# A four-layer graph network: layer 0's denominators on all rows of a head, its outputs divided on the way out of PSUM

## The chip, the cores and the metric

The kernel runs on one core of a Trainium2 chip. The metric is the device time of one execution in microseconds. The median of three runs before the change is 3496.96 us (3496.95 to 3499.22).

## The reference

32 graphs of 512 nodes with 256 features, `x[32,512,256]`, and an adjacency `adj[32,512,512]` of zeros and ones, symmetric, with ones on the diagonal. Four layers follow each other, each as `x = layernorm(x + layer(x, adj))`. Layer 0 is what matters here (4 heads of 64 features; of its five edge types only type 1 occurs):

```python
h = einsum('bnd,hde->bhne', x, W)
weight = mask * (e_src[..., :, None] + e_dst[..., None, :])   # e_src, e_dst = h @ a_src, h @ a_dst
weight = where(adj == 0, NEG, leaky_relu(weight, 0.01))
attention = softmax(weight, axis=-1)
dst = einsum('bhij,bhje->bhie', attention, h) + bias
out = relu(dst) + h
out = per-head layernorm(out) * gamma + beta
```

Layer 1 is graph attention with ELU and one head, layer 2 a masked transformer block (8 heads of 32, feed forward 256 to 1024 to 256), layer 3 graph attention with one head and a leaky slope of 0.2. Everything is f32.

## The kernel before, in words

A graph's 512 nodes stand as R = 4 blocks of P = 128 rows; its features are D = 256 = K x 128 with K = 2. `graph(b)` is a Python generator that emits one graph's instructions, layer after layer, and yields between small units. Each unit has a place: `paced` (before each unit) yields `PERIOD * b + PLACES[stage][i]`, and `heapq.merge` over the 32 generators emits the units in the order of these places. PE's instructions stay in the order of emission (`manual_schedule` for PE). The other engines' orders are the tile framework's: its scheduler plans each engine's queue when the kernel is built, and the queues are then fixed. So a change of `PLACES` moves units of different graphs against each other on PE, and the other engines' queues follow. About seven graphs are in flight at a time. A unit whose place is lower than the current one is emitted at once: layer 0's first four (negative) places are that.

Buffers: PSUM has eight banks, one pool (`bank`). SBUF has a rotating pool for rows of 128x512 (`part`, nine buffers in stages of kind "a", to which layers 0 and 1 belong): gathered rows `gb`, masked weights `pt`, copies `back`, and layer 1's temporaries share it.

Layer 0 (`layer0`), for one graph:

- `h0p` (L104 in the profile, as every PE instruction goes through `product`): x times the weights, four row blocks. ACT takes three exponentials and a copy of each (L427 to L430). `hv[p, j, head, 0:64]` becomes (h + bias) times exp(0.01 e_dst), and column 64 of a head (`HC = 65`) that exponential itself (L431, L436 on DVE).
- `along` (`gp`): for each of four heads, PE transposes a broadcast column so that exp(-0.99 e_src) stands along the rows; ACT copies it out as `gb` (L349).
- Four steps over source blocks j: DVE makes the masked weights `pt` of the four heads, `max(gb, f) * at` (L407, `kept`), each 128x512. PE multiplies them: for each head two matmuls with 32 stationary columns (features 0 to 31 and 32 to 63) into `ops`, and then for each head one with 32 columns into `den`. A matmul of 32 columns writes 32 rows of a bank, and its place in the array (0, 32, 64 or 96) is where those rows begin. Before, a head's two matmuls go to rows 0 and 32, or 64 and 96, of one bank: heads 0 and 1 in the first bank, 2 and 3 in the second. The `den` matmul reads the last 32 columns of the head's 65, and only its last row is the denominator.
- ACT copies the three banks (`back`, L464). PE transposes them back in three units of four (`backp`): first `den`, of which DVE takes the reciprocals (L477), then the two output banks, which DVE divides while it takes the relu (L484).
- DVE adds h (L493), then the per-head layernorm (`head_layernorm`: L293 to L302 and ACT L299), gamma, x, and the layernorm over the row (`layernorm`, ACT L280).

`den` is also the name of attention's denominators in the profile (`den<-pr,ones`), `o` that of layers 1 and 3 (`o<-h,pt`). `s` and `cp` are attention's scores and products, `pr` its probabilities, L663 the adds of halves of `pr` for its denominators, `wop` the projection, `qkp` and `vp` q, k and v, `f1p` and `f2p` the feed forward. L680 adds `wop` to the residual, L273 and L274 are a layernorm's statistics (bn and their aggregation), L276 its shift, L560 the low part of q or k.

`rd` and `mvs` hold denominators' reciprocals and variances of a graph; four small DVE instructions at a graph's end (L825 to L829) check their bounds, on which a fallback path depends.

Of the kernel before, what the change touches and what calls it, by code (L numbers as in the profile page):

```python
# [9 lines left out]
F32 = mybir.dt.float32  # L10
# [4 lines left out]
ALU = mybir.AluOpType  # L15
# [11 lines left out]
PERIOD = 12054  # L27
PLACES = {
    "edges": [-3978, -1720, -957, -79],
    "x": [5375],  # L30
    "mask": [14366, 15324, 18155, 20933],
    "layer 0": [
        -33568, -33515, -33424, -32942, 5301, 7043, 7043, 7043, 8766, 10194, 11091, 11128,
        11993, 11993, 14391,
    ],
    "layer 1": [15460, 15460, 15555, 15555, 15555, 15555, 16382, 17321, 17344, 17344, 17355, 17355],
    "qkv": [18153, 18153, 22255, 22255, 23139, 24065, 25534, 25534, 25534, 25534, 25534],
    "attention": [
        -5960, -4506, -4506, -3927, 26460, 26497, 26497, 26593, 26886, 27435, 27446, 27462,
        28434, 28434, 28779, 29106, 29409, 30200, 31616, 32371, 34290, 34290,  # L40
    ],
    "projection": [34382, 34412, 34412, 34412, 34443],
    "feed forward": [
        36011, 36047, 37566, 38431, 38431, 38519, 38519, 38646, 38646, 38732, 38732, 39499,
        39499, 39646, 39646, 40873, 41200, 41449, 41464,
    ],
    "layer 3": [44919, 44919, 44969, 44969, 44969, 44969, 45682, 48065, 48065, 48065, 48422, 48422],
}
STAGES = {"edges": "a", "x": "a", "layer 0": "a", "layer 1": "a", "feed forward": "c", "layer 3": "c"}
ALL = mybir.DependencyInfo(mybir.DependencyClass.Sync, mybir.DependencyReason.DATA)  # L50
# [22 lines left out]
def fast_path(ctx: ExitStack, tc: tile.TileContext, a: dict, out: bass.AP, bad: bass.AP):  # L73
# [18 lines left out]
    NF = F // P  # L92
    QSCALE = DH**-0.5
    HC = HO + 1
    ND = R * (H + 2)
    NL = 6
    NV = R * (NL + H) + 2 * K

    nc.scalar.preload_act_table_set("natural_log_exp_and_others")
    const = ctx.enter_context(tc.tile_pool(name="const", bufs=1))  # L100
# [307 lines left out]
        return t  # L408


    def layer0(x, xt, at, rd, mv, var):
        h = buf([P, R, D], "h", "h0", 2)
        values = hv[:, :, :, :HO]
        ex = buf([P, 2, H, R], "ex", "ex0", 2)
        for r in range(R):
            yield
            p = bank("h0p")
            for k in range(K):
                product(nc.tensor.matmul,
                    p[:, : D + 2 * H],  # L420
                    xt[:, k, r * P : (r + 1) * P],
                    w0[:, k, :],
                    start=k == 0,
                    stop=k == K - 1,
                )
            s, d = p[:, D : D + H], p[:, D + H : D + 2 * H]
            nc.scalar.activation(ex[:, 0, :, r], s, AF.Exp, scale=-0.99)  # L427
            nc.scalar.activation(hv[:, r, :, HO], d, AF.Exp, scale=0.01)
            nc.scalar.activation(ex[:, 1, :, r], d, AF.Exp, scale=0.99)
            nc.scalar.copy(h[:, r, :], p[:, :D])  # L430
        nc.vector.tensor_add(  # L431
            values,
            h.rearrange("p r (h e) -> p r h e", h=H),
            bias0.rearrange("p (h e) -> p h e", h=H).unsqueeze(1).to_broadcast([P, R, H, HO]),
        )
        nc.vector.tensor_mul(values, values, hv[:, :, :, HO:].to_broadcast([P, R, H, HO]))  # L436
        gbs = []
        for hh in range(H):
            gbs.append((yield from along(ex[:, 0, hh, :].unsqueeze(2), "gb0")))
        den, *ops = (bank(name) for name in ("den0", "o0", "o0"))  # L440
        for j in range(R):
            pt = [kept("pt0", gbs[hh], at[:, j, :], ex[:, 1, hh, j : j + 1]) for hh in range(H)]
            yield
            for hh in range(H):
                for e in range(0, HO, DH):
                    product(nc.tensor.matmul,
                        ops[hh // 2][hh % 2 * HO + e : hh % 2 * HO + e + DH, :],
                        hv[:, j, hh, e : e + DH],
                        pt[hh],
                        start=j == 0,  # L450
                        stop=j == R - 1,
                    )
            for hh in range(H):
                product(nc.tensor.matmul,
                    den[hh * DH : (hh + 1) * DH, :],
                    hv[:, j, hh, HC - DH :],
                    pt[hh],
                    start=j == 0,
                    stop=j == R - 1,
                )  # L460
        back = []
        for i, o in enumerate((den, *ops)):
            t = part("back")
            nc.scalar.copy(t, o)  # L464
            back.append(t)
        y = sb.tile([P, R, D], F32, tag="y", name="y0", bufs=3)
        for i in range(1 + H // 2):
            yield
            p = bank("backp")
            for r in range(R):  # L470
                product(nc.tensor.transpose,
                    p[:, r * P : (r + 1) * P], back[i][:, r * P : (r + 1) * P], ident
                )
            if i == 0:
                rdh = rd.rearrange("p (i r h) -> p i r h", i=H // 2, r=R)
                for i in range(H // 2):
                    nc.vector.reciprocal(  # L477
                        rdh[:, i],
                        p.rearrange("p (r h e) -> p r h e", r=R, h=H)[
                            :, :, 2 * i : 2 * i + 2, DH - 1  # L480
                        ],
                    )
                continue
            nc.vector.scalar_tensor_tensor(  # L484
                y[:, :, (i - 1) * P : i * P].rearrange("p r (h e) -> p r h e", h=2),
                p.rearrange("p (r h e) -> p r h e", r=R, h=2),
                0.0,
                rdh[:, i - 1].unsqueeze(3).to_broadcast([P, R, 2, HO]),
                op0=ALU.max,
                op1=ALU.mult,  # L490
            )
        nc.vector.tensor_add(x, x, all_rows(bet0))
        nc.vector.tensor_add(y, y, h)  # L493
        head_layernorm(y, 1e-6, var)
        nc.vector.tensor_mul(y, y, all_rows(gam0))
        nc.vector.tensor_add(y, y, x)
        layernorm(y, 1e-5, mv[0])
        return y
# [257 lines left out]
        layernorm(x, 1e-5, mv[5])  # L756
        return x

    ends = [0, R * H, R * (H + 1), ND]
    def load_x(b):  # L760
        xt = sb.tile([P, K, N], F32, tag="xt0", name="xt0", bufs=1)
        nc.sync.dma_start(xt, a["xt"][b].rearrange("(k p) n -> p k n", p=P))
# [4 lines left out]
        nc.sync.dma_start(x, a["x"][b].rearrange("(r p) d -> p r d", p=P))  # L767
        return xt, x

    def layer0_all(b, x, xt, at, rd, mv, var):  # L770
        if b == 0:
            bcast(bet0, "bet0")
            bcast(gam0, "gam0")
        return (yield from layer0(x, xt, at, rd, mv, var))

    def layer1_all(b, x, at, rd, mv):
        if b == 0:
            weights13(w1g, "w1g", "a1")
        return (yield from layer1(x, at, rd, mv))
# [22 lines left out]
    def graph(b):  # L802
        yield PERIOD * b + PLACES["edges"][0]
        rd = sb.tile([P, ND], F32, tag="rd", name="rd", bufs=3)
        mvs = sb.tile([P, 2 * NL * R + H * R + 2 * K], F32, tag="mvs", name="mvs", bufs=3)
        mv = [mvs[:, 2 * i * R : 2 * (i + 1) * R].rearrange("p (r s) -> p r s", s=2) for i in range(NL)]
        tops = mvs[:, 2 * NL * R :]
        var, spread = tops[:, : H * R], tops[:, H * R :]
        rds = [rd[:, ends[i] : ends[i + 1]] for i in range(3)]
        if b == 0:  # L810
            xt, x = yield from paced(b, "x", load_x(b))
        at = yield from paced(b, "edges", mask(b))
        if b:
            xt, x = yield from paced(b, "x", load_x(b))
        x = yield from paced(b, "layer 0", layer0_all(b, x, xt, at, rds[0], mv, var))
        x = yield from paced(b, "layer 1", layer1_all(b, x, at, rds[1], mv))
        a2 = yield from paced(b, "mask", symmetric(b, at))
        qk = yield from paced(b, "qkv", qkv_all(b, x))
        ct = yield from paced(b, "attention", attention(qk, *a2, spread))
        y = yield from paced(b, "projection", attended_all(b, x, ct))  # L820
        x = yield from paced(b, "feed forward", feed_forward_all(b, x, y, mv))
        x = yield from paced(b, "layer 3", layer3_all(b, x, at, rds[2], mv))
        nc.sync.dma_start(out[b].rearrange("(r p) d -> p r d", p=P), x)
        okd, oks, okv = ok[:, :ND], ok[:, ND : ND + NL * R], ok[:, ND + NL * R :]
        nc.vector.scalar_tensor_tensor(okd, rd, RD_MIN, okd, op0=ALU.is_ge, op1=ALU.mult)  # L825
        nc.vector.scalar_tensor_tensor(okd, rd, RD_MAX, okd, op0=ALU.is_le, op1=ALU.mult)
        variances = mvs[:, 1 : 2 * NL * R : 2]
        nc.vector.scalar_tensor_tensor(oks, variances, VAR_MAX, oks, op0=ALU.is_le, op1=ALU.mult)
        nc.vector.scalar_tensor_tensor(okv, tops, VAR_MAX, okv, op0=ALU.is_le, op1=ALU.mult)  # L829
# [664 lines left out]
```

## Time and profile before

| What | Value |
|---|---|
| Median of three runs | 3496.96 us |
| The profiled execution, and its span | 3497.4 us, 3495.6 us |
| Granted TensorE clock, mean | 0.986 |
| DVE pt (L407), 128x512 | 768 of 742 ns |
| DVE add of halves (L663), 128x1024 | 384 of 1208 ns |
| DVE y + h (L493), 128x1024 | 32 of 1225 ns |
| DVE division with relu (L484), 128x512 from PSUM | 64 of 686 ns |
| DVE multiply (L611), 128x512 | 64 of 683 ns |
| DVE reciprocal of a bank's denominators (L477) | 64 of 175 ns |
| ACT copy of `den`, of `o` (L464), 128x512 | 32 of 585 ns, 64 of 595 ns |
| ACT Copy, Ln, Exp of attention's denominators (L606, L607, L608) | 64 each of 600, 637, 635 ns; reading the accumulator 196 and 199 ns more for L606 and L608 |
| DMA issue to landing: x, xt, adj, adjt | 5.1, 3.8, 5.0, 3.9 us |

A group in the profile is a line, an engine, an operation and tiles (out<-in), with the count, the busy time of all together and the mean duration of one; behind the bar stands how long its engine was idle before it and what ended that. Records on PE may overlap, so busy time is less than count times mean. In a timeline the columns are start, length, engine, line, operation, tiles, and how many instructions were merged. A matmul in f32 leaves two records, a transpose one.

### The profile page before, as it was taken

The page shows a single profiled execution, that of the slowest core. Times are in us where ns is not written, and L with a number is a line of the kernel's source. Part 1 is how long each engine was busy: PE and PEld are TensorE (multiplying, and loading weights), DVE is VectorE, ACT ScalarE, POOL GpSimd, SP SyncE. Part 2 cuts the span into 40 slices and gives each one's busy share as a digit, 9 for nine tenths or more (in the row PEclk, how much of TensorE's full clock was granted, in tenths as well). Part 3 has the DMA queues.
Part 4 walks back from the last instruction along what each step waited for, and adds up shares of the span by engine and source line. Part 5 has one row for each costly group of instructions (what it writes and reads, how often), then busy time and mean ns, then how long its engine had stood idle before and what let it go on. Part 6 is the DMA issues. An engine that isn't in the chain of part 4 may idle for free.

```text
span 3495.6 us, 51507 instructions
## 1 busy us (share of the span) xinstructions
PE 3397.5 (97%) x18342; PEld 2366.5 (68%) x18342; DVE 2888.4 (83%) x5178; ACT 2223.0 (64%) x5729; POOL 82.0 (2%) x171
## 2 busy tenths in 40 slices
PE   5799999999999999999999999999999999999986
PEld 3466667776667776667776667776666776666765
DVE  5778888888888888889888889888889888889863
ACT  3556667666667666667666667666667666666652
POOL 0000000000000000000000000000000000000000
PEclk8899999999999999999999999999999999999998
DMA  4334232333232333232333232334332333332220
GB/s 131 85 76 91 61 85 59 81 79 91 62 84 61 79 79 91 64 85 61 76 79 91 67 82 63 74 79 91 69 80 66 71 79 91 71 79 61 45 55 13
DMA packets 164038, 261.01 MB, mean 75 GB/s; under 512 B 20416, under 2 KB 56384, under 8 KB 163776
## 3 DMA queue, kind: packets, MB, share of 16 engines
q1 hardware_dynamic: 163776, 257.65, 32.0%
q8 instruction: 148, 2.42, 0.3%
q14 instruction: 114, 0.93, 0.1%
HBM read 106.57 MB, written 16.78 MB: 35 GB/s over the span
## 4 chain that ended last, share of the span: by engine, by line
PE 94%; DVE 3%; ACT 1%; issue 1%; DMA 1%; SPq 0%; POOL 0%; DVEq 0%; ACTq 0%; POOLq 0%
PE o L104 20%; PE f2p L104 13%; PE f1p L104 13%; PE s L104 8%; PE qkp L104 6%; PE cp L104 6%; PE den L104 5%; PE h3p L104 4%; PE wop L104 3%; PE h1p L104 3%; PE vp L104 3%; PE h0p L104 3%; PE gp L104 2%; PE backp L104 1%; PE xt3p L104 1%
## 5 line engine op out<-in xcount | busy, mean ns | idle before, releaser
L636 DVE TENSOR_TENSOR pr<-pr,a 128x1024 f32<-128x1024 f32 x384 | 454.7, 1217 | 185.4 <-ACT pr L633 185.4
L407 DVE SCALAR_TENSOR_TENSOR pt<-gb,ex,at 128x512 f32<-128x512 f32 x768 | 536.7, 742 | 42.0 <-ACT gb L349 31.6
L633 ACT ACTIVATE pr<-s 128x512 f32<-128x512 f32 x1024 | 545.3, 616 | 3.0 <-PE s L104 3.0
L104 PE MATMUL f2p<-wf,ft 128*128 128x256 f32 x2048 | 484.8, 379 | 5.4 <-ACT ft L706 5.2
L104 PE MATMUL f1p<-yt,wf 128*128 128x256 f32 x2048 | 483.8, 379 | 0.0
L104 PE MATMUL o<-h,pt 128*128 128x257 f32 x2048 | 476.5, 382 | 4.5 <-DVE pt L407 4.4
L104 PEld LDWEIGHTS o<-h,pt 128*128 128x128 f32 x2048 | 386.4, 190 | 99.1 <-issue 44.2
L663 DVE TENSOR_TENSOR pr<-pr 128x1024 f32<-128x1024 f32 x384 | 446.8, 1208 | 2.8 <-PE cp L104 2.8
L104 PEld LDWEIGHTS f2p<-wf,ft 128*128 128x128 f32 x2048 | 383.9, 190 | 63.4 <-ACT ft L706 9.8
L104 PEld LDWEIGHTS f1p<-yt,wf 128*128 128x128 f32 x2048 | 388.5, 190 | 55.0 <-DVE lo L560 0.5
L280 ACT ACTIVATE y<-y,rs 128x256 f32<-128x256 f32 x768 | 398.0, 593 | 17.1 <-DVE rs L276 17.1
L104 PE MATMUL s<-qk 128*128 128x512 f32 x1024 | 377.4, 470 | 4.6 <-DMA qk<-lo 3.8
L706 ACT ACTIVATE ft<-f1p,cols 128x256 f32<-128x256 f32 x512 | 217.0, 469 | 236.6 <-PE f1p L104 235.6
L273 DVE BATCH_NORM_STATS2 bn<-y 128x6 f32<-128x256 f32 x768 | 298.9, 410 | 5.6
L104 PE MATMUL o<-pt,hv 128*32 128x512 f32 x2048 | 286.5, 607 | 8.0 <-DVE pt L407 8.0
L265 ACT ACTIVATE rs<-mvs,eps1e-05_70 128x4 f32<-128x4 f32 x192 | 57.5, 300 | 326.7 <-DVE mvs L274 319.6
L104 PE MATMUL qkp<-xt,wqkv 128*128 128x512 f32 x512 | 240.5, 603 | 0.0
L104 PE MATMUL cp<-pr,v 128*32 128x512 f32 x2048 | 234.2, 595 | 1.4 <-DVE pr L636 1.4
L104 PEld LDWEIGHTS s<-qk 128*128 128x128 f32 x1024 | 189.3, 192 | 55.8 <-issue 27.7
L104 PEld LDWEIGHTS o<-pt,hv 128*32 128x32 f32 x2048 | 73.3, 110 | 179.6 <-issue 94.1
L559 ACT ACTIVATE hi<-qkp,cols 128x512 fp32r<-128x512 f32 x128 | 88.4, 691 | 164.1 <-PE qkp L104 162.1
L752 DVE RECIPROCAL rd<-o 128x1 f32<-128x1 f32 x128 | 21.5, 168 | 177.7 <-PE o L104 177.5
(139 smaller groups left out, 4881.9 us busy)
## 6 DMA issues: line engine op xcount, KB each, us to landing
qk<-hi SPq DMA_DIRECT2D x512, 128.0 KB, 3.4
qk<-lo SPq DMA_DIRECT2D x512, 128.0 KB, 3.5
adjt<-in_adjt SPq DMA_DIRECT2D x64, 512.0 KB, 3.9
adj<-in_adj SPq DMA_DIRECT2D x64, 512.0 KB, 5.0
xt<-in_xt SPq DMA_DIRECT2D x32, 512.0 KB, 3.8
x<-in_x SPq DMA_DIRECT2D x32, 512.0 KB, 5.1
out<-y SPq DMA_DIRECT2D x32, 512.0 KB, 4.5
wf<-in_w1t SPq DMA_DIRECT2D x1, 1024.0 KB, 9.8
```

The source lines that it names most:

```text
L104: latest[0] = what(*args, **kwargs).ins.name
L265: nc.scalar.activation(out, variance, AF.Ln, bias=eps[e])
L273: nc.vector.bn_stats(st[:, r, :], y[:, r, :])
L280: nc.scalar.activation(y[:, r, :], y[:, r, :], AF.Identity, bias=rs[:, 1, r : r + 1], scale=rs[:, 0, r : r + 1],)
L407: nc.vector.scalar_tensor_tensor(t, g, f, edges, op0=ALU.max, op1=ALU.mult)
L559: nc.scalar.activation(hi, p, AF.Identity, bias=bias)
L633: nc.scalar.activation(t[:, i, :], s, AF.Exp, scale=QSCALE)
L636: nc.vector.tensor_mul(t, t, edges)
L663: nc.vector.tensor_add(t, t, u)
L706: nc.scalar.activation(ft[:, f, :], p[:, f, :], AF.Relu, bias=bf1[:, ff + f : ff + f + 1])
L752: nc.vector.reciprocal(rd[:, r : r + 1], p[:, D : D + 1])
```

## The change

The two matmuls of a head now write the same 32 rows (those of the head) of the two output banks, so that features 0 to 31 of all heads stand in one bank and 32 to 63 in the other. The denominator's matmul has the column 64 of the head broadcast to 32 stationary columns: all 32 rows of a head in `den` are its denominator, and `den` lies like either output bank. ACT takes exp(-ln(den)) of the whole bank (`inv`), DVE multiplies both output banks by it as it moves them to SBUF, and PE transposes only these two. The relu and the addition of h are one DVE instruction, with strided views (`halves`). The bounds are checked on sums that ACT accumulates (`spread0`) instead of on 16 reciprocals. `mvs` has four buffers instead of three. Every list in `PLACES` is new, with one unit less in layer 0.

```diff
 PLACES = {
-    "x": [5375],
-    "mask": [14366, 15324, 18155, 20933],
+    "x": [6086],
+    "mask": [14366, 15398, 19563, 21001],
     "layer 0": [
-        -33568, -33515, -33424, -32942, 5301, 7043, 7043, 7043, 8766, 10194, 11091, 11128,
-        11993, 11993, 14391,
+        -36153, -36100, -36009, -36009, 2373, 3347, 3347, 3351, 8768, 10196, 11113, 11130,
+        13480, 14393,
     ],
...
-    "projection": [34382, 34412, 34412, 34412, 34443],
+    "projection": [34462, 34462, 35198, 35198, 35294],
...
             for hh in range(H):
                 for e in range(0, HO, DH):
                     product(nc.tensor.matmul,
-                        ops[hh // 2][hh % 2 * HO + e : hh % 2 * HO + e + DH, :],
+                        ops[e // DH][hh * DH : (hh + 1) * DH, :],
                         hv[:, j, hh, e : e + DH],
                         pt[hh],
...
                 product(nc.tensor.matmul,
                     den[hh * DH : (hh + 1) * DH, :],
-                    hv[:, j, hh, HC - DH :],
+                    hv[:, j, hh, HO:].to_broadcast([P, DH]),
                     pt[hh],
...
+        inv = part("inv")
+        nc.scalar.activation(inv, den, AF.Ln)
+        nc.scalar.activation(inv, inv, AF.Exp, scale=-1.0, accum_out=spread0[:, 1:2])
         back = []
-        for i, o in enumerate((den, *ops)):
+        for o in ops:
             t = part("back")
-            nc.scalar.copy(t, o)
+            nc.vector.tensor_mul(t, o, inv)
             back.append(t)
+        nc.scalar.activation(inv, den, AF.Copy, accum_out=spread0[:, 0:1])
...
-        for i in range(1 + H // 2):
+        for i in range(2):
             yield
             p = bank("backp")
             for r in range(R):
                 product(nc.tensor.transpose,
                     p[:, r * P : (r + 1) * P], back[i][:, r * P : (r + 1) * P], ident
                 )
-            if i == 0:
-                rdh = rd.rearrange("p (i r h) -> p i r h", i=H // 2, r=R)
-                for i in range(H // 2):
-                    nc.vector.reciprocal(...)
-                continue
             nc.vector.scalar_tensor_tensor(
-                y[:, :, (i - 1) * P : i * P].rearrange("p r (h e) -> p r h e", h=2),
-                p.rearrange("p (r h e) -> p r h e", r=R, h=2),
+                halves(y, i),
+                p.rearrange("p (r h e) -> p r h e", r=R, h=H),
                 0.0,
-                rdh[:, i - 1].unsqueeze(3).to_broadcast([P, R, 2, HO]),
+                halves(h, i),
                 op0=ALU.max,
-                op1=ALU.mult,
+                op1=ALU.add,
             )
         nc.vector.tensor_add(x, x, all_rows(bet0))
-        nc.vector.tensor_add(y, y, h)
         head_layernorm(y, 1e-6, var)
...
-        mvs = sb.tile([P, 2 * NL * R + H * R + 2 * K], F32, tag="mvs", name="mvs", bufs=3)
+        mvs = sb.tile([P, 2 * NL * R + H * R + 2 * K + 2], F32, tag="mvs", name="mvs", bufs=4)
```

The order of each engine's instructions in the two built kernels differs as follows, around layer 0 of one graph in the middle of the run. On PE: all four `gp` of layer 0 stand together after `h0p` (before, four scores stood after the first); `wop` is split, two row blocks, then the third `qkp`, then two row blocks, then the steps j=2 and j=3 (before, all of `wop` and then `qkp`); after layer 3's third row block come `ytp`, the fourth row block, `ytp`, `qkp`, two `vp`, `f1p`, the first `backp`, two `vp`; the second `backp` comes earlier by some 60 records of the feed forward and the scores. On DVE: the four pt of j=0 come before all six adds L663 (before, one add stood ahead of them); the four pt of j=3 come after the add of `wop`'s last block, one aggregation, and with one bn, one aggregation, a check and L276 between them; the two multiplies (`back`) follow j=3's pt, and behind them stand the third L560 and layer 3's reciprocals. On ACT: Ln and Exp follow the feed forward's layernorm, then the third `hi` of q and k, the Copy, and `yt`.

More of the change, by code (lines that the diff above doesn't have):

```diff
@@ L29 @@
     "edges": [-3978, -1720, -957, -79],
-    "x": [5375],
-    "mask": [14366, 15324, 18155, 20933],
+    "x": [6086],
+    "mask": [14366, 15398, 19563, 21001],
     "layer 0": [
-        -33568, -33515, -33424, -32942, 5301, 7043, 7043, 7043, 8766, 10194, 11091, 11128,
-        11993, 11993, 14391,
-    ],
-    "layer 1": [15460, 15460, 15555, 15555, 15555, 15555, 16382, 17321, 17344, 17344, 17355, 17355],
-    "qkv": [18153, 18153, 22255, 22255, 23139, 24065, 25534, 25534, 25534, 25534, 25534],
+        -36153, -36100, -36009, -36009, 2373, 3347, 3347, 3351, 8768, 10196, 11113, 11130,
+        13480, 14393,
+    ],
+    "layer 1": [15517, 15517, 15564, 15564, 15564, 15564, 16391, 17330, 17353, 17353, 17353, 17353],
+    "qkv": [15645, 15645, 22398, 22398, 23141, 24048, 25474, 25474, 25557, 25557, 25557],
     "attention": [
-        -5960, -4506, -4506, -3927, 26460, 26497, 26497, 26593, 26886, 27435, 27446, 27462,
-        28434, 28434, 28779, 29106, 29409, 30200, 31616, 32371, 34290, 34290,
+        -5988, -5975, -4578, -3999, 26439, 26452, 26497, 26593, 27411, 27448, 27448, 27464,
+        28436, 28436, 28781, 29108, 29411, 30202, 31600, 31618, 34292, 34292,
     ],
-    "projection": [34382, 34412, 34412, 34412, 34443],
+    "projection": [34462, 34462, 35198, 35198, 35294],
     "feed forward": [
-        36011, 36047, 37566, 38431, 38431, 38519, 38519, 38646, 38646, 38732, 38732, 39499,
-        39499, 39646, 39646, 40873, 41200, 41449, 41464,
+        36011, 36092, 37566, 38486, 38486, 38519, 38519, 38646, 38646, 38732, 38732, 39510,
+        39510, 39648, 39648, 41202, 41202, 41451, 41466,
     ],
-    "layer 3": [44919, 44919, 44969, 44969, 44969, 44969, 45682, 48065, 48065, 48065, 48422, 48422],
+    "layer 3": [44890, 44890, 44940, 44940, 44940, 44940, 46119, 47665, 47665, 47665, 48119, 48119],
 }
@@ L94, in fast_path @@
     HC = HO + 1
-    ND = R * (H + 2)
+    ND = R * 2
     NL = 6
-    NV = R * (NL + H) + 2 * K
+    NV = R * (NL + H) + 2 * K + 2
     nc.scalar.preload_act_table_set("natural_log_exp_and_others")
@@ L408, in kept, with layer0 @@
         return t
-    def layer0(x, xt, at, rd, mv, var):
+    def layer0(x, xt, at, spread0, mv, var):
         h = buf([P, R, D], "h", "h0", 2)
@@ L460, in layer0, with halves @@
                 )
+        inv = part("inv")
+        nc.scalar.activation(inv, den, AF.Ln)
+        nc.scalar.activation(inv, inv, AF.Exp, scale=-1.0, accum_out=spread0[:, 1:2])
         back = []
-        for i, o in enumerate((den, *ops)):
+        for o in ops:
             t = part("back")
-            nc.scalar.copy(t, o)
+            nc.vector.tensor_mul(t, o, inv)
             back.append(t)
+        nc.scalar.activation(inv, den, AF.Copy, accum_out=spread0[:, 0:1])
         y = sb.tile([P, R, D], F32, tag="y", name="y0", bufs=3)
-        for i in range(1 + H // 2):
+        def halves(t, i):
+            return t.rearrange("p r (h i e) -> p r h i e", h=H, i=2)[:, :, :, i]
+        for i in range(2):
             yield
@@ L473, in layer0 @@
                 )
-            if i == 0:
-                rdh = rd.rearrange("p (i r h) -> p i r h", i=H // 2, r=R)
-                for i in range(H // 2):
[L477 to L482, printed above, removed]
-                continue
             nc.vector.scalar_tensor_tensor(
-                y[:, :, (i - 1) * P : i * P].rearrange("p r (h e) -> p r h e", h=2),
-                p.rearrange("p (r h e) -> p r h e", r=R, h=2),
+                halves(y, i),
+                p.rearrange("p (r h e) -> p r h e", r=R, h=H),
                 0.0,
-                rdh[:, i - 1].unsqueeze(3).to_broadcast([P, R, 2, HO]),
+                halves(h, i),
                 op0=ALU.max,
-                op1=ALU.mult,
+                op1=ALU.add,
             )
         nc.vector.tensor_add(x, x, all_rows(bet0))
-        nc.vector.tensor_add(y, y, h)
         head_layernorm(y, 1e-6, var)
@@ L757, in layer3 @@
         return x
-    ends = [0, R * H, R * (H + 1), ND]
+    ends = [0, R, ND]
     def load_x(b):
@@ L768, in load_x, with layer0_all @@
         return xt, x
-    def layer0_all(b, x, xt, at, rd, mv, var):
+    def layer0_all(b, x, xt, at, spread0, mv, var):
         if b == 0:
@@ L773, in layer0_all @@
             bcast(gam0, "gam0")
-        return (yield from layer0(x, xt, at, rd, mv, var))
+        return (yield from layer0(x, xt, at, spread0, mv, var))
     def layer1_all(b, x, at, rd, mv):
@@ L808, in graph @@
         var, spread = tops[:, : H * R], tops[:, H * R :]
-        rds = [rd[:, ends[i] : ends[i + 1]] for i in range(3)]
+        rds = [rd[:, ends[i] : ends[i + 1]] for i in range(2)]
         if b == 0:
@@ L814, in graph @@
             xt, x = yield from paced(b, "x", load_x(b))
-        x = yield from paced(b, "layer 0", layer0_all(b, x, xt, at, rds[0], mv, var))
-        x = yield from paced(b, "layer 1", layer1_all(b, x, at, rds[1], mv))
+        x = yield from paced(b, "layer 0", layer0_all(b, x, xt, at, spread[:, 2 * K :], mv, var))
+        x = yield from paced(b, "layer 1", layer1_all(b, x, at, rds[0], mv))
         a2 = yield from paced(b, "mask", symmetric(b, at))
@@ L821, in graph @@
         x = yield from paced(b, "feed forward", feed_forward_all(b, x, y, mv))
-        x = yield from paced(b, "layer 3", layer3_all(b, x, at, rds[2], mv))
+        x = yield from paced(b, "layer 3", layer3_all(b, x, at, rds[1], mv))
         nc.sync.dma_start(out[b].rearrange("(r p) d -> p r d", p=P), x)
```

## The prediction, before the result was known

> **What bounds the kernel now.** I read the page first: busy shares, the chain that ended last, the costliest groups.
>
> ```profile
> PE 3397.5 (97%) x18342; PEld 2366.5 (68%) x18342; DVE 2888.4 (83%) x5178; ACT 2223.0 (64%) x5729; POOL 82.0 (2%) x171
> ...
> PE 94%; DVE 3%; ACT 1%; issue 1%; DMA 1%; SPq 0%; POOL 0%; DVEq 0%; ACTq 0%; POOLq 0%
> ...
> L104 PE MATMUL o<-pt,hv 128*32 128x512 f32 x2048 | 286.5, 607 | 8.0 <-DVE pt L407 8.0
> ```
>
> PE is the chain. The last line says how the 32-column matmuls of layer 0 run: 2048 x 607 ns is 1243 us of records in 286.5 us of busy time, 4.3 at once. A matmul on 32 columns uses one of four column strips of the array (the strip is where the output begins in its bank: rows 0, 32, 64, 96), and four strips stream side by side. Each f32 matmul leaves two records (1024 matmuls, 2048 records).
>
> Next, the busy time in a window of one graph, from one xt1 transpose to the next (busy columns: PE, PEld, DVE, ACT, POOL):
>
> ```profile
> 1499.50:1604.13 104.63, 104.63 (x573) 73.45 (x572) 89.70 (x162) 69.35 (x180) 2.49 (x5) 1.00 0.33 76
> ```
>
> PE never looks idle: a graph costs 104.63 us of PE, at full clock, and what PE's order loses or gains per graph comes 32 times. A busy PE can still be half filled, so I took PE's timeline through layer 0's four steps over j:
>
> ```profile
> 1534.41 2.31 PE L104 MATMUL o<-pt,hv 128*32 128x512 f32 x14
> 1536.32 0.60 PE L104 MATMUL den<-pt,hv 128*32 128x512 f32 x2
> 1536.55 0.60 PE L104 MATMUL o<-pt,hv 128*32 128x512 f32 x2
> 1536.75 1.26 PE L104 MATMUL den<-pt,hv 128*32 128x512 f32 x6
> 1537.94 3.75 PE L104 MATMUL h3p<-w3g,xt 128*128 128x258 f32 x16
> ...
> 1543.82 1.90 PE L104 MATMUL o<-pt,hv 128*32 128x512 f32 x16
> ...
> 1546.50 3.70 PE L104 MATMUL qkp<-xt,wqkv 128*128 128x512 f32 x8
> ...
> 1553.67 1.88 PE L104 MATMUL qkp<-xt,wqkv 128*128 128x512 f32 x4
> 1555.48 1.93 PE L104 MATMUL o<-pt,hv 128*32 128x512 f32 x16
> 1557.22 1.04 PE L104 MATMUL den<-pt,hv 128*32 128x512 f32 x8
> 1558.08 2.08 PE L104 MATMUL o<-pt,hv 128*32 128x512 f32 x16
> ...
> 1560.95 5.48 PE L104 MATMUL o<-h,pt 128*128 128x257 f32 x24
> ...
> 1567.14 1.04 PE L104 MATMUL backp<-ident,back 128*128 128x128 f32 x8
> 1568.01 1.02 PE L104 MATMUL qkp<-xt,wqkv 128*128 128x512 f32 x2
> ```
>
> A step is 24 records. The eight den records from 1557.22 to 1558.08 take 0.86 us, so a round of four strips is 0.43 us and a step six rounds, 2.58 us. Step j=1 (1543.82 to 1546.50) takes 2.68: full speed and 0.1 for changing the tile size. Step j=0 takes 3.53 and the pair j=2, j=3 5.47 where 5.26 would do: there PE waits inside for pt, the masked weights of one head. DVE's timeline over the same stretch:
>
> ```profile
> 1532.13 1.18 DVE L663 TENSOR_TENSOR pr<-pr 128x1024 f32<-128x1024 f32 x1
> ...
> 1533.98 2.06 DVE L407 SCALAR_TENSOR_TENSOR pt<-gb,ex,at 128x512 f32<-128x512 f32 x3
> 1535.97 5.75 DVE L663 TENSOR_TENSOR pr<-pr 128x1024 f32<-128x1024 f32 x5
> 1541.64 2.72 DVE L407 SCALAR_TENSOR_TENSOR pt<-gb,ex,at 128x512 f32<-128x512 f32 x4
> ...
> 1553.22 1.41 DVE L680 TENSOR_TENSOR y<-wop,y 128x256 f32<-128x256 f32 x4
> ...
> 1557.64 1.41 DVE L407 SCALAR_TENSOR_TENSOR pt<-gb,ex,at 128x512 f32<-128x512 f32 x2
> ```
>
> The last head's pt ends at 1536.04 (j=0), 1544.37 (j=1) and 1559.06 (j=3). Where it is the limit, the run ends 1.90 later both times (1537.94, 1560.95): two rounds of o for that head, two of den, and about 0.18 of wakeup and size change.
>
> **The change, part by part.**
>
> Transposes. Four of twelve per graph go. Eight take 0.87 us in the same timeline (1567.14 to 1568.01), 0.109 each: 4 x 0.109 = 0.44 us a graph, all on PE. The group's busy time is the upper bound, 137 ns each and 0.55:
>
> ```profile
> L104 PE MATMUL backp<-ident,back 128*128 128x128 f32 x384 | 52.5, 273 | 1.4 <-ACT back L464 1.4
> ```
>
> The strips, which the diff does not announce. Before, the two matmuls of a head go to neighbouring strips (rows 0 and 32 of one bank, or 64 and 96), so a late head holds two strips for two rounds. After, they go to the *same* strip of two banks: a head is one strip for four rounds, then its den for two. With all four pt there the step is still six rounds, if the queue looks past a strip's waiting matmuls. With a late last head it ends six rounds after that pt, not four: 1.90 becomes 1.90 + 0.86 = 2.76.
>
> Does the queue look ahead? The den records at 1536.32 began before the last o records (1536.55), which stand ahead of them in the program, so strips do overtake. After, PE must pass up to twelve records to start the fourth strip at once. How far it can is not shown; I take it as enough, because the overtaking shown has no visible delay, and price the other case below.
>
> The Trainium skill speaks against that, "TensorE: Matmul & The Clock Gate", Part 3, "The mechanism": matmuls are "strict FIFO, no reordering". By this rule a step would take 13 rounds before (5.6 us) and 17 after: 1.7 us more for each of 128 steps, an estimate of +220 us. The rows above (2.68 us, and den ahead of o) disagree, and the measurement decides.
>
> Now the three runs, laid out with the order the changed kernel is built to.
>
> j=0: one L663 that stood before the four pt moves behind them. The last pt ends 1.15 earlier (5.75 / 5), at 1534.9; end 1534.9 + 2.76 = 1537.66, against 1537.94: -0.28.
>
> j=1: DVE runs without a gap from L663 at 1532.13 to here and does the same instructions before the last pt in both kernels, so it ends at 1544.37 again. PE's run ends at 1544.37 + 2.76 = 1547.13 instead of 1546.50: +0.63, whatever j=0 gained. Here a run that was at full speed becomes limited by pt.
>
> j=2, j=3: in the new places qkp stands between the halves of wop, so the last wop ends just before j=2 instead of 1.81 earlier. DVE's order then is: add of wop's last row (done about 0.6 after j=2's start: PE's tail 0.16, wakeup, 0.41 for the add), an aggregation, four pt with the last bn and small ones between. Before, from the last add (1554.63) to the last pt (1559.06) was 4.43, of which bn and aggregation from 1554.55 to 1556.07 were 1.52; now one bn and one aggregation (0.48) stand there: 4.43 - 1.52 + 0.48 = 3.4. The last pt ends 0.6 + 3.4 = 4.0 after the start of j=2 (3.58 before), the run 4.0 + 2.76 = 6.76 after it, against 5.47: +1.29.
>
> Division and wait. ACT: three copies (L464, 0.585 to 0.595) go, 1.78; Ln, Exp and Copy come, by attention's rows L607 (0.64), L608 (0.635 + 0.2 for the accumulator) and L606 (0.6 + 0.2), 2.28. ACT is busy 69 of 104.6 us: hidden. DVE: L493's add (1.225) and two reciprocals (0.35) go, two multiplies (0.69, as L611 and L484) come: -0.2, no gain, since that add stood after the backs, where PE had other work. The new wait: DVE's multiplies wait for ACT's Exp, and behind them in DVE's queue stand qk's third lo and layer 3's reciprocals and scalings. Chain from den's end: 0.64 + 0.84 + 2 x 0.69 = 2.9 us. PE needs the first freed bank after three o3 rows, 5.3 us (1560.95 to 1566.27); DVE itself idles 3.9 us there (to 1562.99). Cover 2.4 us; without it at most 2.9 a graph. Taken as nothing.
>
> The rest. x's load, gp, the second half of adj, two ytp and the backs move. A period of 12054 places is 104.63 us; the late adj half is now issued 21001 - 19563 = 1438 places, 12.5 us, before its use, and lands in 5.0; x stands further ahead. On SP's queue the late adj half passes no qk transfer by its new place. Changing to and from transposes costs no start time (T to 256 columns: 0.109). Narrower checks, the fourth mvs buffer: nothing. Ramp: the first layer 0 has bare chains; within 3 us either way.
>
> Sum per graph: -0.44 + 0.63 + 1.29 = +1.48 us; 32 x 1.48 = +47. The profiled execution is 3497.4 us (span 3495.6), 0.4 above the median 3497.0; 3497 + 47 = 3544.
>
> **Rivals.**
>
> *Only the transposes count* (faster). If pt come early enough that all runs are at PE's rate or better, the tails vanish: 32 x -0.44 = -14 (-18 by busy time): 3483, and down to 3470 if j=0 gains half of its 0.85 too. For it: PE is the chain, and j=0 does get pt earlier. Against: DVE is gapless there, with the same work. It decides if j=1's last pt ends before about 1543.7 and j=3's within 2.7 us of j=2's start.
>
> *The queue is too short* (slower still). If a strip's pending matmul stops dispatch until its predecessor's second pass begins, heads start 0.43 apart, 1.29 for the fourth: j=0 ends 1534.41 + 1.29 + 2.69 = 1538.39 (+0.45), j=1 starts at 1544.27 and ends at 1548.25 (+1.75), j=2/3 stays at 6.76 (+1.29): 1.75 + 1.29 - 0.44 = +2.6, 3580. For it: overtaking by more than a few records is shown nowhere in these lines. Against: no delay in what is shown.
>
> *The division's chain shows* (slower): up to +2.9 a graph on top, 3590 to 3637. Only if the 2.4 us of cover is gone.
>
> **How the numbers follow.** Likeliest, pt-limited tails: 0.56, 3544, by itself 3515 to 3562 (j=1 between 0.2 and 0.9, j=3 between 0.8 and 1.7). Short queue 0.15, chain 0.04: slower 0.75. Transposes alone: faster 0.20. Tails that just cancel them: 0.05. The measurement can tell about 0.2%, 7 us. The range reaches down over the faster case and up over the short queue: 3475 to 3590.
>
> **What would show it.** Right: the graph's window grows to about 106.1; j=1's run is near 3.3 us and j=2/3 near 6.8; each run ends 2.7 to 2.8 after its last pt; backp x256. Wrong: j=1 at 2.7 and a window of 104.2 (the faster rival); heads starting 0.43 apart with all pt present (short queue); PE idle with releaser DVE back L467 (the chain).

## The result, and the profile after

The changed kernel takes 3532.15 us (median of 4 runs, 3529.67 to 3535.43) against 3496.95 beside it: ratio 1.010, 95% interval 1.0082 to 1.0117. It is slower by 35 us; the forecast was slower by 47. The profiled execution took 3535.43 us, its span is 3533.7, the granted clock 0.986 as before.

From the page of the changed kernel, the busy shares and the costliest group of layer 0's steps:

```profile
PE 3433.2 (97%) x18150; PEld 2397.5 (68%) x18214; DVE 2877.7 (81%) x5146; ACT 2236.0 (63%) x5793; POOL 81.3 (2%) x171
...
L104 PE MATMUL o<-pt,hv 128*32 128x512 f32 x2048 | 320.0, 606 | 7.4 <-DVE pt L407 7.4
```

DVE has become less busy and PE more, with 128 transposes fewer (another 64 matmul records are missing from this trace; the weight loads are all there). The second line says where: the same 2048 records of the same length (606 ns, before 607) now fill 320.0 us instead of 286.5, so 3.9 run at once instead of 4.3. (More than four are possible on four strips, because a record of 592 ns overlaps the next on its own strip, which starts 430 ns after it.)

One graph in the window view of the changed kernel (columns as in the prediction):

```profile
1411.62:1517.38 105.76, 105.69 (x567) 74.23 (x568) 89.35 (x161) 69.73 (x182) 2.50 (x5) 1.00 0.35 75
```

105.75 us a graph on the mean of eight windows against 104.63: +1.12, and 32 x 1.12 = 36 us is the whole loss. PE's timeline of the changed kernel shows which steps carry it:

```profile
1553.19 1.95 PE L104 MATMUL o<-pt,hv 128*32 128x512 f32 x16
...
1555.92 3.75 PE L104 MATMUL h3p<-w3g,xt 128*128 128x258 f32 x16
...
1561.80 2.01 PE L104 MATMUL o<-pt,hv 128*32 128x512 f32 x15
1563.52 0.64 PE L104 MATMUL den<-pt,hv 128*32 128x512 f32 x3
1563.65 0.59 PE L104 MATMUL o<-pt,hv 128*32 128x512 f32 x1
...
1565.03 3.70 PE L104 MATMUL qkp<-xt,wqkv 128*128 128x512 f32 x8
...
1573.83 1.94 PE L104 MATMUL o<-pt,hv 128*32 128x512 f32 x16
...
1579.12 1.33 PE L104 MATMUL den<-pt,hv 128*32 128x512 f32 x3
1580.38 1.79 PE L104 MATMUL o<-h,pt 128*128 128x257 f32 x7
```

j=1 (1561.80 to 1565.03) takes 3.23 us instead of 2.69, j=2 with j=3 (1573.83 to 1580.38) 6.55 instead of 5.47; j=0 (1553.19 to 1555.92) now runs at full speed, 2.73 instead of 3.53. DVE's timeline of the changed kernel gives the ends of the last pt of j=0, j=1 and j=3, and the first division:

```profile
1552.08 0.74 DVE L407 SCALAR_TENSOR_TENSOR pt<-gb,ex,at 128x512 f32<-128x512 f32 x1
...
1559.56 2.72 DVE L407 SCALAR_TENSOR_TENSOR pt<-gb,ex,at 128x512 f32<-128x512 f32 x4
...
1576.88 0.74 DVE L407 SCALAR_TENSOR_TENSOR pt<-gb,ex,at 128x512 f32<-128x512 f32 x1
1581.87 0.69 DVE L467 TENSOR_TENSOR back<-o,inv 128x512 f32<-128x512 f32 x1 [4.24 <-ACT inv L463]
```

The last pt of j=1 and j=3 end at 1562.28 and 1577.62, and both runs end 2.75 us later (1565.03, 1580.38). In the kernel before it was 1.90. The 4.24 us that DVE waits for `inv` look bad and cost nothing, as a run below shows. The groups with shapes kept apart confirm the transposes:

```profile
L104 PE MATMUL backp<-ident,back 128*128 128x128 f32 x256 | 39.2, 277 | 3.1 <-DVE back L467 3.1
```

PE's time from the first record of a group to that of the next, in us per graph (mean of eight), before and after:

| Group | Before | After | Difference |
|---|---|---|---|
| `cp` | 7.14 | 8.04 | +0.89 |
| layer 0's four steps | 11.69 | 12.51 | +0.81 |
| `backp` | 1.23 | 0.79 | -0.44 |
| `f2p`, `f1p`, `s`, `gp`, `qkp`, `wop` | | | +0.19, -0.18, +0.11, -0.09, -0.09, -0.08 |
| graph | 104.63 | 105.75 | +1.12 |

`cp` was in no term of the prediction. ACT's timeline of the changed kernel shows why it is late:

```profile
1547.42 2.08 ACT L280 ACTIVATE y<-y,rs 128x256 f32<-128x256 f32 x4
1549.40 0.57 ACT L349 COPY gb<-gp 128x512 f32<-128x512 f32 x1
1549.86 0.61 ACT L630 ACTIVATE pr<-s 128x512 f32<-128x512 f32 x1
```

With all `gp` ahead of the four scores, the exponentials of the last scores (L630) stand behind four rows of a layernorm and a copy, and one of the two `cp` stretches waits inside (4.53 us for 32 records instead of 3.64); a run below, with three `gp` behind the scores, confirms it. It comes back at once: DVE's last pt of j=0 ends at 1552.82, so PE, arriving at 1553.19, finds all four.

### The profile page after: what moved, and what is told of

Read it like the earlier page. It is cut to its first block, busy times and chain, and to the rows that moved or that the text cites. A ratio compares the mean times of both kernels' runs of the same rounds, so it can differ in the third digit from the quotient of the medians.

```text
span 3533.7 us, 51217 instructions
## 1 busy us (share of the span) xinstructions
PE 3433.2 (97%) x18150; PEld 2397.5 (68%) x18214; DVE 2877.7 (81%) x5146; ACT 2236.0 (63%) x5793; POOL 81.3 (2%) x171
## 4 chain that ended last, share of the span: by engine, by line
PE 95%; DVE 3%; ACT 1%; DMA 0%; issue 0%; SPq 0%; ACTq 0%; DVEq 0%
PE o L104 20%; PE f2p L104 13%; PE f1p L104 12%; PE s L104 8%; PE cp L104 7%; PE qkp L104 6%; PE den L104 5%; PE h3p L104 3%; PE h1p L104 3%; PE wop L104 3%; PE vp L104 3%; PE h0p L104 3%; PE gp L104 2%; PE xt3p L104 1%; PE xt1p L104 1%; PE backp L104 1%
## 5 line engine op out<-in xcount | busy, mean ns | idle before, releaser
L630 ACT ACTIVATE pr<-s 128x512 f32<-128x512 f32 x1024 | 550.2, 616 | 5.8 <-PE f2p L104 2.2
L280 ACT ACTIVATE y<-y,rs 128x256 f32<-128x256 f32 x768 | 398.3, 593 | 13.1 <-DVE rs L276 13.0
L104 PE MATMUL o<-pt,hv 128*32 128x512 f32 x2048 | 320.0, 606 | 7.4 <-DVE pt L407 7.4
L104 PE MATMUL cp<-pr,v 128*32 128x512 f32 x2048 | 259.5, 596 | 0.3 <-DVE pr L633 0.3
L104 PEld LDWEIGHTS o<-pt,hv 128*32 128x32 f32 x2048 | 102.3, 110 | 152.3 <-issue 135.7
L104 PE MATMUL den<-pt,hv 128*32 128x512 f32 x1024 | 201.7, 593 | 0.0
L104 PEld LDWEIGHTS cp<-pr,v 128*32 128x32 f32 x2048 | 67.3, 109 | 152.2 <-issue 116.6
```

The costliest lines, as they stand in the source:

```text
L104: latest[0] = what(*args, **kwargs).ins.name
L280: nc.scalar.activation(y[:, r, :], y[:, r, :], AF.Identity, bias=rs[:, 1, r : r + 1], scale=rs[:, 0, r : r + 1],)
L630: nc.scalar.activation(t[:, i, :], s, AF.Exp, scale=QSCALE)
```

## The experiments

The theory is the prediction's: a head on one strip makes a run end 2.75 us after its last pt instead of 1.90. The rivals that were left: the new places cost the time (above all `cp`), or the division's chain does. The ratios are to the kernel before, run beside each on the same chip. "Runs" are the durations of j=0, of j=1, and of j=2 with j=3, in this order; "window" is the mean time of a graph, from one xt1 to the next.

**The strips alone, in the kernel before.**

```diff
-                        ops[hh // 2][hh % 2 * HO + e : hh % 2 * HO + e + DH, :],
+                        ops[e // DH][hh * DH : (hh + 1) * DH, :],
```

(and the reciprocals and the division read by matching views)

> The kernel before with one thing changed: a head's two matmuls write the same 32 rows of two banks (the new layout), with the divide's views adapted; places, copies, three transposed banks and instruction counts stay. Strips theory (a late head holds one strip for six rounds, so a run ends 2.75 us after its last pt and not 1.90): j=0's run 4.38 us instead of 3.53, j=1 unchanged at 2.69, j=2/3 6.0 to 6.33 instead of 5.47; +1.35 to +1.7 us a graph, 3540 to 3552 us. Places theory (the loss comes from the new places, the layout is neutral): 3497, runs as before. Division-chain theory: 3497.

3544.85 us, 1.0143 (1.0126 to 1.016). The runs take 4.38, 2.73 and 6.30, a limited run ends 2.75 after its last pt, and layer 0's steps are 1.72 us a graph longer. One edit of where a matmul writes costs more than the whole change.

**The new places alone, in the kernel before.**

```diff
-PLACES = { (before) }
+PLACES = { (after) }
```

> The kernel before with the places of the changed one, nothing else. Strips theory: cp grows by 0.9 (the last scores come late), j=0's run shrinks to 2.7 (its pt are all there), j=1 2.69, j=2/3 3.8 + 1.9 = 5.7: about +0.2 us a graph, 3497 to 3505 us. Places theory: the whole loss and the four transposes on top, about +1.5 a graph, 3545 us. Division-chain theory: 3497.

3629.56 us, 1.0383 (1.0366 to 1.04): none of the theories had it. Layer 0's runs are as the strips theory says (2.71, 2.69, 5.70, and 1.90 after the last pt; 0.59 less a graph), and yet a graph takes 109.22 us. The group of xt1's transposes, which open the next layer, shows the wait, here in the kernel with the new places alone:

```profile
L104 PE MATMUL xt1p<-ident,y 128*128 128x128 f32 x256 | 63.5, 338 | 69.9 <-ACT y L280 69.7
```

and here in the changed kernel:

```profile
L104 PE MATMUL xt1p<-ident,y 128*128 128x128 f32 x256 | 36.5, 283 | 23.5 <-ACT y L280 23.3
```

Layer 0's tail on DVE runs from the backs to the last layernorm's rows (ACT y, L280). With the old body (three banks back, and L493 behind them) these rows end 45.8 us after the last step, with the new body 41.2; the new places ask for xt1 at 42.8. So body and places of the change belong together, and this tail is the next limit behind the steps.

The wait has a price behind it too. Against the changed kernel, a graph loses 3.1 us ahead of and inside xt1, and another 1.3 in `f2p`. A window of this kernel over the eight `f2p` records just behind xt1 shows why (the granted clock, 1.00 in the changed kernel's window above, is 0.59 here):

```profile
900.77:903.83 3.06, 3.06 (x8) 2.53 (x9) 3.06 (x6) 2.24 (x5) 0.00 (x0) 0.59 0.00 0
```

These eight records take 3.06 us, in the kernel before 1.72. By the trace's clock record the clock is at half for 3.41 us once a graph from 463 to 3194 us, in 26 graphs, and no other kernel of this case has such a stretch between 210 and 3300 us. How long a wait it takes is not shown.

**The new body alone, with the places of before.**

```diff
 # kernel after
-PLACES = { (after) }
+PLACES = { (before, layer 0 one unit shorter) }
```

> The changed kernel with the places of the one before (one unit of layer 0 fewer). Strips theory: j=0 4.38, j=1 2.69, j=2/3 6.0 to 6.33, transposes -0.44: +0.9 to +1.3 a graph, 3526 to 3538 us. Places theory: only the transposes count, 3483. Division-chain theory: the loss stays as in the changed kernel, 3530, but with runs over j as before and PE waiting for the backs or for a bank.

3540.44 us, 1.0127 (1.0111 to 1.0144), 2 us above what the strips theory allowed. Runs 4.40, 2.73 and 6.30 (+1.73 a graph), `backp` -0.44, `wop` -0.18, `f2p` +0.09: the window is 105.85, and 32 x 1.22 is 39 us; the other 6 us lie in the first graphs and were not taken apart. The new places are not what slows the change: with them the window is 0.1 us shorter and the time lower by 8 us, over two sets of runs.

**j=1 later, in the changed kernel.**

```diff
-        ... 8768, 10196, 11113, 11130,
+        ... 8768, 10345, 11113, 11130,
```

> The changed kernel with one place changed: layer 0's step j=1 after the first two qkp (10345 instead of 10196), so that its last pt is there 3.5 us before it is needed. Strips theory: j=1's run falls from 3.22 to 2.73 and the graph by 0.3 to 0.5 us, if j=2's pt do not wait for j=1's buffers: 3516 to 3523 us, against 3532 for the changed kernel. Places or division-chain theory: 3532.

3555.75 us, 1.0173 (1.0156 to 1.019): a miss. j=1 does run at full speed (2.73), but in DVE's new order three adds of halves instead of two stand ahead of the end of layer 0's tail, and DVE waits 1.0 us for ACT before L302, where the changed kernel's does not wait. The tail's last rows now end at 43.2 us instead of 41.2, and xt1 takes 0.95 us a graph longer. A place that cures one wait moved another.

**The strips undone, in the changed kernel.**

```diff
-                        ops[e // DH][hh * DH : (hh + 1) * DH, :],
+                        ops[hh // 2][hh % 2 * HO + e : hh % 2 * HO + e + DH, :],
```

> The changed kernel with one line undone: a head's two output matmuls go to neighbouring strips again, as before the change. The division still takes the denominators of its own rows, so three heads in four are divided by another head's denominators; the work and every queue's order stay those of the changed kernel. Strips theory: the last pt come when they did, but a run ends 1.90 us after them instead of 2.75. j=1: its last pt ended 0.48 after its start, so it runs at full speed, 2.69 instead of 3.23 (-0.54); j=2 and j=3: 3.79 + 1.90 = 5.69 instead of 6.55 (-0.86); j=0 stays at 2.7. Sum -1.40 us a graph: window near 104.4, 3532 - 45 = 3487 us (3480 to 3498). Places or division theory (the loss comes from the new places or from the wait for the division, not from the strips): 3528 to 3536, unchanged.

3486.32 us (3484.99 to 3488.15, 8 runs), 0.9969 (0.9958 to 0.998). This kernel leaves out the right division (six of the eight halves of heads take another head's denominators), so it serves for its time alone. PE's timeline of it, j=2 and j=3:

```profile
1550.52 1.92 PE L104 MATMUL o<-pt,hv 128*32 128x512 f32 x16
...
1554.84 1.45 PE L104 MATMUL den<-pt,hv 128*32 128x512 f32 x7
1556.22 2.00 PE L104 MATMUL o<-h,pt 128*128 128x257 f32 x8
```

and the last pt in its DVE timeline:

```profile
1553.57 0.75 DVE L407 SCALAR_TENSOR_TENSOR pt<-gb,ex,at 128x512 f32<-128x512 f32 x1
```

The last pt ends 3.80 after the start, as in the changed kernel, and the run 1.90 later. Layer 0's steps fall by 1.41 us a graph, every other group stays within 0.01, the window is 104.33; 32 x 1.41 = 45 us, and the medians of the two kernels, from two sets of runs, lie 45.8 apart. This settles the cause: all of the loss, and more, is the strip.

**Two strips a head with the right denominators.** Half 32 to 63 of head h goes to strip h+2, so the second multiply takes its reciprocals from the other 64 rows.

```diff
-                        ops[e // DH][hh * DH : (hh + 1) * DH, :],
+                        ops[e // DH][(hh * DH + e * 2) % P : (hh * DH + e * 2) % P + DH, :],
...
-            nc.vector.tensor_mul(t, o, inv)
+            if o is ops[0]:
+                nc.vector.tensor_mul(t, o, inv)
+            else:
+                for q in (0, HO):
+                    nc.vector.tensor_mul(t[q : q + HO, :], o[q : q + HO, :], inv[HO - q : P - q, :])
```

(and for the second bank the relu with h as one instruction a head)

> The changed kernel with the second output bank rotated by two strips: features 0 to 31 of head h on strip h, 32 to 63 on strip h+2, so that a head again holds two strips. The second multiply becomes two of 64 rows (the reciprocals come from the other half's rows), and the relu with h of the second bank becomes four small instructions, one a head. Strips theory: the runs of the experiment with the strips undone (2.7, 2.7, 5.7), -1.40 us a graph; DVE has one multiply of 0.69 and about 0.3 more, both behind the steps, which count only if layer 0's last layernorm comes later than xt1p: 3487 if they are hidden, up to 3503 if half a microsecond a graph shows. Rival (the division's chain is the limit): +0.69 + 0.3 a graph on top of the changed kernel, 3564.

3531.33 us, 1.0101 (1.0085 to 1.0118), a miss for both theories. The steps are 1.41 us a graph shorter as expected, but xt1 is 1.44 longer. DVE's timeline of this kernel shows the tail:

```profile
1701.39 0.89 DVE L489 SCALAR_TENSOR_TENSOR y<-backp,h 128x128 f32<-128x128 f32 x4
...
1711.83 1.23 DVE L302 TENSOR_TENSOR y<-y,st 128x1024 f32<-128x1024 f32 x1 [1.33 <-ACT st L266]
...
1715.04 1.21 DVE L500 TENSOR_TENSOR y<-y,x 128x1024 f32<-128x1024 f32 x1
1716.16 1.22 DVE L667 TENSOR_TENSOR pr<-pr 128x1024 f32<-128x1024 f32 x1
```

Four instructions of 0.89 us together where one of 0.69 stood cost little themselves, but they change DVE's order: it now waits 1.33 us for ACT before L302, where the changed kernel's order leaves no wait, and another add of halves (L667) stands between y and its layernorm. The rows end 2.4 us later than in the changed kernel.

**Three `gp` behind the scores, in the changed kernel.**

```diff
-        ... 2373, 3347, 3347, 3351, 8768, ...
+        ... 2373, 6095, 6095, 6095, 8768, ...
```

> The changed kernel with three of layer 0's gp units behind the four scores, as before the change, so that ACT takes the last scores' exponentials ahead of the four y rows. Theory that attention's products (cp, 8.04 us against 7.14 before) are a loss of their own: cp returns to 7.14, window 104.9, 3532 - 28 = 3504. Strips theory: DVE's gapless stretch up to the last pt of j=1 sets the end, so what cp gives back j=0 takes (its run is then 4.4 as in the two same-strip kernels with the places of before, with 2.75 after the last pt) and j=1 comes out at 2.7: cp + j=0 + j=1 was 8.04 + 2.73 + 3.23 = 14.00 and becomes 7.14 + 4.40 + 2.73 = 14.27: window 105.8 to 106.0, 3532 to 3542.

3541.06 us, 1.0126 (1.0109 to 1.0143). `cp` falls to 7.14 and j=0 rises to 4.39, 2.75 after its last pt; j=1 takes 2.73. The window is 106.01, the upper end of what the strips theory said. The loss in `cp` was no loss of its own: DVE's stretch up to j=1's last pt sets that end.

**A longer chain for the division, in the changed kernel.**

```diff
         nc.scalar.activation(inv, den, AF.Ln)
+        for _ in range(2):
+            nc.scalar.copy(inv, inv)
```

> The changed kernel with two more passes of ACT over the 128x512 logarithms (copies in place, about 0.6 us each), between Ln and Exp: the division's chain is 1.2 us longer at least. The scheduler puts the third hi of q and k ahead of the second pass, and the multiplies behind layer 3's first scaling and the third lo. Hidden-division theory: PE's first freed bank is needed 5.3 us after the run, the longer chain ends at 4.1 to 5.1: nothing, 3529 to 3540. Rival (the division's wait is on the path): 1.2 to 2.2 us a graph, 3570 to 3602.

3533.1 us, 1.0105 (1.0088 to 1.0122), window 105.73. From the groups of this kernel:

```profile
L469 DVE TENSOR_TENSOR back<-o,inv 128x512 f32<-128x512 f32 x64 | 41.0, 682 | 12.0 <-ACT inv L465 12.0
...
L464 ACT COPY inv<-inv 128x512 f32<-128x512 f32 x64 | 39.2, 612 | 1.0
```

39.2 us of ACT more, and the multiplies end 5.0 us after the step instead of 2.8: nothing. The chain is off the path with at least 2.2 us to spare.

**Two strips, rows returned by the multiply.** As *two strips a head* above, but the multiply moves the output back to its rows, and layer 0's tail stays as in the change.

```diff
 # kernel with two strips a head
-                    nc.vector.tensor_mul(t[q : q + HO, :], o[q : q + HO, :], inv[HO - q : P - q, :])
+                    nc.vector.tensor_mul(t[q : q + HO, :], o[HO - q : P - q, :], inv[q : q + HO, :])
```

(and the relu with h as in the changed kernel)

> As the kernel with two strips a head (second bank rotated by two strips), but the two multiplies of 64 rows write the rows back to their places, so that the relu with h is one instruction a bank again, and layer 0's tail on DVE is the changed kernel's. Strips theory, with the last run's extra wait put down to that tail: layer 0's runs 2.71, 2.69, 5.70 (11.10 a graph against 12.51), xt1p 0.87 instead of 2.31, the extra multiply of 0.69 hidden as the longer chain was: window 104.3, 3486 us (3482 to 3493). Rival (the extra multiply counts): +0.69 a graph, 3508; (any rotation delays xt1p): 3531 again.

3487.24 us (3486.89 to 3488.11, 7 runs) beside 3497.96: 0.9971 (0.9959 to 0.9982). From the groups of this kernel:

```profile
L104 PE MATMUL o<-pt,hv 128*32 128x512 f32 x2048 | 270.0, 603 | 7.6 <-DVE pt L407 7.6
...
L471 DVE TENSOR_TENSOR back<-o,inv 64x512 f32<-64x512 f32 x64 | 44.1, 689 | 1.9
```

4.6 records run at once. The second line is the two multiplies of 64 rows that stand for one of 128; the window of 104.33, that of the kernel with the strips undone, shows that the extra one is hidden. This version beats both kernels: by 11 us the one before, by 45 the change (two sets of runs). It keeps the rest of the change, the broadcast denominators, the division and the places, so none of these is what slows it.

**The same with the places of before.**

```diff
 # kernel with the rows returned
-PLACES = { (after) }
+PLACES = { (before, layer 0 one unit shorter) }
```

> The same kernel with the places of before (layer 0's list one unit shorter). Strips theory: nothing of the loss is left, and of the change only the four transposes and what moved with them: runs as before (3.53, 2.69, 5.47), backp -0.44, f2p +0.10 as in the changed body on these places: window 104.2 to 104.3, 3483 to 3486. Rival (the new places are what makes the kernel with the strips undone faster than before): 3497.

3493.07 us, 0.999 (0.9981 to 0.9999): the window was met, the time was not. Runs 3.54, 2.69 and 5.48 as before, `backp` -0.44, `f2p` +0.09: window 104.31, 0.32 below before, which is 10 us. Only 5 arrive in the time; the rest lies outside the steady graphs and is open. So are the 6 us by which the new places are faster at the same window (3487.24, 104.33). The 0.32 a graph is what the changed body is worth without the shared strip.

**All of wop before the third qkp, with the rows returned.**

```diff
-    "projection": [34462, 34462, 35198, 35198, 35294],
+    "projection": [34462, 34462, 34462, 34462, 35294],
```

> The kernel with the rows returned, and its places changed in one unit pair: all of wop before the third qkp, as before the change, so that DVE has wop's last adds behind it earlier when j=2 starts. Expected: the j=2 and j=3 runs 5.47 (as before) instead of 5.70, wop 0.08 more: window 104.15 to 104.2, 3480 to 3483. Rival (DVE now takes the layernorm's statistics ahead of the pt, so nothing is gained): 3486.

3488.09 us, 0.9969 (0.9958 to 0.9981): not to be told from the kernel it started from, and above the 3480 to 3483 expected. j=2 with j=3 take 5.48 as expected, qkp 0.09 more; the window is 104.24, which makes 3 us in 32 graphs, and in the profiled executions the first xt1 comes 2.5 us later.

## Why the prediction was right or wrong

Direction and mechanism were right: a head on one strip ends its run later, and two runs are limited by it. The size was 12 us too large. By its steps:

- Transposes, -0.44: measured -0.437, in the change and in the new body alone.
- The tail of a late head, 2.76 instead of 1.90: measured 2.75 where a head has one strip and 1.90 where it has two, in every kernel whose run is limited by its last pt. That the queue looks far enough was assumed, and was right: in the changed kernel, with all pt there, the four heads of j=0 start at 1553.191, .204, .218 and .231, 13 ns apart, where the short queue would have them 430 apart. The rule of the Trainium skill that the prediction weighed ("TensorE: Matmul & The Clock Gate", Part 3, "The mechanism", strict order) does not agree with these starts.
- j=0 and j=1, +0.63 at j=1's end: measured `cp` +0.89, j=0 -0.80, j=1 +0.54, together +0.63. The sum was right because DVE's gapless stretch sets this end; its parts were not, so its exactness is partly luck. j=0's own -0.28 missed that `cp` would come late, since ACT's order around the moved `gp` was not followed.
- j=2 and j=3, +1.29: measured +1.08. This is the term that was mis-sized: the last pt comes 3.79 us after j=2's start, not 4.0 (the last add is done after 0.53, not 0.6, and the last pt 3.26 after it, not 3.4). 0.21 a graph is 7 us.
- "The rest" at nothing: the small groups of the table sum to -0.16 a graph before rounding, 5 us. With the 7 that is the 12.
- Division at nothing: right, and shown by the longer chain. Its price without cover, up to 2.9 us a graph, did not fall due.

The sum was +1.48 a graph; it is +1.12. Of the rivals, *only the transposes count* named the right condition: where the runs reach PE's rate or the old tail, as with the rows returned, the change is a gain. It failed because j=1 and j=3 are limited by pt, which the prediction held against it: the last pt of j=3 came 3.79 us after j=2's start, and the rival needed 2.7.

## What to carry to other kernels

When several column strips share PE, ask which strips a late operand holds, because its matmuls on one strip follow each other after it has come. Here two strips instead of one for a head's two output matmuls save 0.85 us after each late operand (1.90 against 2.75); more than two were not tried. Read the busy time of such a group against count times mean; a fall in records at once is lost PE time that the share of 97% hides. Before a place is moved on the engine that sets the end, follow the other engines' queues as far as the next consumer: here a wait cured at one step came back at xt1 three times, once with half the clock behind it.

## What was not expected of the hardware

DVE's multiply of 64 rows, with its PSUM rows shifted by 64 against its output, takes 689 ns, and the multiply of 128 rows in place 692 in the same kernel: half the rows, moved to the other half, took as long as all of them. What the shift and the number of rows each do alone is not shown. Matmuls waiting one behind another on a strip do not hold up the other three: in the changed kernel's j=1, three `den` records begin from 1563.52 on, ahead of the `o` at 1563.65 that stands before them in the program.
